# A wait ahead of each indirect DMA: GpSimd issues a fetch or scatter only when the one two places ahead has landed

## The chip, the core and the metric

The kernel runs on one core of a Trainium2 chip. The metric is the device time of one execution in microseconds, as the median of several timed runs. A profile is one further execution, taken with the hardware profiler. The engines are named as the profile names them: PE is TensorE, DVE is VectorE, ACT is ScalarE, POOL is GpSimd and SP is SyncE, which here only issues DMAs.

## What is computed

The input x holds two images of 256 channels and 64 x 64 = 4096 positions, in float32. Two layers follow one another. Cut to what matters:

```
# layer 0
y   = prelu(batchnorm(conv3x3(x)))            # 64 channels
e   = y.reshape(B, 64, N)                     # N = 4096
sim = einsum('bdn,bdm->bnm', e, e)            # 4096 x 4096 for each image
p   = sparsemax(sim, axis=2)                  # max(sim - tau, 0), tau for each row
x   = einsum('bcn,bnm->bcm', x, p) + x
# layer 1
g   = g_w @ x + g_b                           # 128 channels, at each position
a   = w_t . (theta_w @ x + theta_b)           # one number at each position
b   = w_p . (phi_w @ x + phi_b)
f   = relu(a[:, None] + b[None, :] + wf_b)    # 4096 x 4096
y   = (f / N) @ g
x   = batchnorm(wz_w @ y + wz_b) + x
```

In layer 1, f is never needed as a matrix: row n of the product is the sum of (a_n + b_m) g_m over those m with b_m > -a_n. If the positions are sorted by b and running sums of g and b·g are kept in that order, each row is one look-up in the table of sums.

## The kernel before

**A planner orders the work.** Each image passes through the convolution, the search for rows of sim that have more than one entry above the threshold, the rows themselves, the attention product, the projections to g, a and b, and layer 1. The kernel does not write the order down by hand. It describes tasks with `plan.task(cost, fn, rank, after, lat=..., take=..., free=...)`: `cost` has the engine (P, D, A, G for PE, DVE, ACT, POOL; S for SP) and an assumed duration in us, `lat` is an assumed time from its end until others can use the result, `take` and `free` hold a place in a ring of buffers. `Plan.run` plays the tasks through on a clock of its own. On each engine it takes, among the open tasks, the one that could start earliest; when several could start at once, the one of lowest `rank`. Instructions are emitted in the order in which the planner starts them, and each engine runs its own instructions in that order. Costs and ranks so fix the order of the instructions only; on the chip semaphores decide when each one starts. The ranks are the twenty numbers of L281: DB for the mask products on POOL, CV1 for image 1's convolution, RW0 and RW1 for the rows, A0 and A1 for the attention products, R0 and R1 for the sort keys, K0 and K1 for the counting, CH0 and CH1 for the table and the fetches, P1, P2 and SP1 for image 1's projections, PY and PF for its direct product.

**Layer 1 by sorting (class `Ranked`).** Image 0 sorts all 32 tiles of 128 positions, image 1 the first 16; image 1's other 16 tiles go by the direct product (`pair_f` on ACT, L1427; `pair_py` on PE, L1435; `pair_rest`, L1446).

- `above` (L1032 on ACT, L1037 on DVE) and `ties` (L1051) count for each position how many keys come before it; `place` (L1066) turns four tiles' counts into ranks, the `rank` tile.
- `scatter` (L1072) writes a tile's 128 rows of 130 numbers to their ranks in the DRAM table `sg`, by an indirect DMA of POOL. A memset of the one-element tile `gap` (L1071) stands ahead of each. There are 32 for image 0 and 16 for image 1, in groups of four as `place` gives them out. All scatters of an image are declared independent of one another.
- `load` (L1087) brings the sorted table back, `products` (L1098), `sums` (L1105), `before` (L1109) and `raised` (L1112) make the running sums, `stored` (L1118) writes them to the DRAM table `tb`.
- `segments` (L1132, L1133), `places` (L1141) and `counts` (L1150 to L1153) find for each position its place in the table, the tile `k`.
- `fetch` (L1158) is an indirect DMA of POOL which gathers 128 rows of 257 numbers (128 x 257 x 4 bytes) from `tb` into one of the 16 places of the tile `r`. There are 32 for each image. The first 16 of an image follow the stored table; each later one is made a task when the place it overwrites has been used (`taken`, L1192).
- `taken` consumes the fetched rows in blocks of four: `scaled_sums` (L1171, DVE) combines the two halves of a row in place, `turned` (L1178, PE) transposes it, L1183 (image 0, ACT) or L1185 (image 1, DVE) makes `yT`, and `finish` multiplies by wz (`pz`, L956), adds into x (L960, DVE) and stores the block (L963, SP).

POOL also squares conv outputs, makes part of image 1's convolution inputs, multiplies x by a mask (L764, `doubled`) and issues the fetches of the listed rows (L710, L714). In all cases it runs its instructions one after another; the indirect DMAs take turns on eight semaphores.

The planner's entries for the two kinds of DMA:

```
self.fetched[t] = plan.task({"G": 1.27}, lambda: self.fetch(t), rank, after, lat=4.14)
...
self.places_done.append(plan.task({"G": 1.28}, lambda i=i: self.scatter(i), ranked, [pl], lat=2.3))
```

Of the kernel before, what the change touches and what calls it, by code (L numbers as in the profile page):

```python
# [8 lines left out]
F32 = mybir.dt.float32  # L9
# [18 lines left out]
CI = 128  # L28
G = 2
EPS = 1e-5  # L30
HALVINGS = 26
KB = 3
UN = 2 * CB
# [7 lines left out]
TH = 16  # L41
# [5 lines left out]
def both_layers(tc, a, out):  # L47

    nc = tc.nc
    with ExitStack() as keep:
        flag = keep.enter_context(tc.tile_pool(name="flag", bufs=1))
        rows_i = flag.tile([1, 1], I32, name="rows_i")
        sparse_path(tc, a, out, rows_i)
        n = nc.values_load(
            rows_i[0:1, 0:1],
            min_val=0,
            max_val=1 << 16,
            skip_runtime_bounds_check_because="a count of rows",  # L60
        )
        with tc.If(n > 0):
            dense_path(
                tc, a["x"], a["conv_w"], a["vec0"], a["g_wt"], a["g_b"], a["theta_w"], a["phi_w"],
                a["vec_ci"], a["wz_wt"], a["vec1"], out,
            )
# [124 lines left out]
def sparse_path(ctx: ExitStack, tc, a, out, rows_i):  # L191
    nc = tc.nc
# [8 lines left out]
    small = ctx.enter_context(tc.tile_pool(name="small", bufs=1))  # L201
# [44 lines left out]
    def weights():  # L246

        nc.vector.tensor_scalar_add(s1, v1[:, 4, :], EPS)
        nc.scalar.activation(s1, s1, AF.Sqrt)
# [28 lines left out]
            nc.tensor.matmul(pc, lhsT=wc[:, kc], rhs=gw_sb[:, kc], start=(kc == 0), stop=(kc == CT - 1))  # L278
        nc.vector.tensor_sub(gb_sb, gb_sb, pc)

    DB, CV1, LS, RW0, SV1, RW1, A0, G0, A1, R0, K0, CH0, R1, K1, CH1, P1, P2, SP1, PY, PF = 13.5, 11.59, -11.38, -21.22, -11.5, -7.77, 14.5, -12.16, -19.33, 14.33, -0.92, -6.33, -24.95, -6.8, -0.35, -15.83, -22.49, -13.59, 6.76, -7.17  # L281
    plan = Plan()
    ring_sim, ring_av, ring_y, ring_b = Ring(3), Ring(2), Ring(2), Ring(2)

# [650 lines left out]
    def spread(name, column, dst, t0, nt, rank, after):  # L935

        rd, t = as_row(name, column, t0, nt, rank, after)

        def go():
            nc.sync.dma_start(out=dst()[:, ds(t0 * P, nt * P)], in_=rd.to_broadcast((P, nt * P)))  # L940

        return plan.task({"S": 0.1}, go, rank, [t], lat=2.27 + nt * 0.1)
# [33 lines left out]
    class Ranked:  # L976
# [90 lines left out]

        def scatter(self, t):
            b = self.b
            gap = small.tile([1, 1], F32, name=f"gap_{b}_{t}", tag="gap")  # L1070
            nc.gpsimd.memset(gap, 0.0)  # L1071
            rows = nc.gpsimd.indirect_dma_start(  # L1072
                out=self.sg,
                out_offset=bass.IndirectOffsetOnAxis(ap=self.rank[:, t : t + 1], axis=0),
                in_=self.ga[:, t, 0 : CI + 2],
                in_offset=None,
            )

            tc.declare_no_dep(rows.ins, group=f"sg{b}", reason="the ranks are a permutation")
            tc.add_to_no_dep_group(f"sg{b}", rows.ins)  # L1080
# [74 lines left out]
        def fetch(self, t):  # L1155
            if t == 0:
                self.r = self.at("r", [P, TH, CS], F32)
            nc.gpsimd.indirect_dma_start(  # L1158
                out=self.r[:, t % TH],
                out_offset=None,  # L1160
                in_=self.tb,
                in_offset=bass.IndirectOffsetOnAxis(ap=self.k[:, t : t + 1], axis=0),
            )
# [31 lines left out]
            finish(b, ds(i * CB, CB), scaled, "A" if rest is None else "D", rank, after, h)  # L1195

        def fetch_task(self, t, rank, after):
            self.fetched[t] = plan.task({"G": 1.27}, lambda: self.fetch(t), rank, after, lat=4.14)

        def begin(self, rank, after, ranked, chained, then, room):  # L1200

            self.chained, self.then = chained, then
            k = plan.task({"D": 1.65}, self.keys, rank, after)
            hz = ring_b.hold()
            plan.task({"G": 0.2}, self.first, rank, [k], lat=2.3, take=hz, free=[hz])
            sp = spread(f"k{self.b}", lambda: self.key, lambda: self.kb, 0, self.R, rank, [k])
            n = self.R * P
            self.places_done, self.ranked, places = [], [], []
            for t in range(self.R):
                r = ranked + t / 100.0  # L1210
                u = plan.task(
                    {"D": 0.25 + 0.00107 * n, "A": 0.66 + 0.00083 * n}, lambda e, t=t: self.above(t, e == "A"), r, [sp, *room]
                )
                self.ranked.append(u)
                places += [u, plan.task({"D": 0.36}, lambda t=t: self.ties(t), r + 0.02, [sp, *room])]
                if t % 4 == 3:
                    pl = plan.task({"D": 0.6}, lambda t=t: self.place(t - 3), ranked - 0.7, places)
                    for i in range(t - 3, t + 1):
                        self.places_done.append(plan.task({"G": 1.28}, lambda i=i: self.scatter(i), ranked, [pl], lat=2.3))
                    places = []  # L1220
            self.chain()

# [45 lines left out]
    def scales():  # L1268
        nc.vector.tensor_scalar_add(s0, v0[:, 4:5], EPS)
        nc.scalar.activation(s0, s0, AF.Sqrt)  # L1270
        nc.vector.reciprocal(s0, s0)
        nc.vector.tensor_mul(s0, s0, v0[:, 1:2])
        nc.vector.tensor_sub(b0, v0[:, 0:1], v0[:, 3:4])
        nc.vector.tensor_mul(b0, b0, s0)
        nc.vector.tensor_add(b0, b0, v0[:, 2:3])
        nc.vector.tensor_scalar_mul(ns0, s0, -1.0)
# [119 lines left out]
    for m0 in range(0, NT, 6):  # L1396
        early = m0 < 17
        rank = P1 if early else P2
# [5 lines left out]
        after = attended if m0 == 0 else [projected[m0 - 1]]  # L1404
        t = plan.task({"P": 0.37 * 2 * (min(m0 + 6, NT) - m0)}, product, rank, after, take=h)
        t = plan.task({"D": 0.9}, lambda d=d: d["out"](), rank, [t], free=[h])
# [14 lines left out]
    f = []  # L1421

    def pair_f(q, m):
        if not f:
            f.append(room.tile([P, 4, UN], F32, name="f", tag="S2"))
        fm, am, bm = f[0][:, m % 4, :], ab1[0][:, ts(q, UN)], ga1[0][:, m, CI : CI + 1]
        nc.scalar.activation(fm, am, AF.Relu, bias=bm)  # L1427
# [22 lines left out]
    for q in range(NU):  # L1450
        hq = ring_sim.hold()
        for m in range(NR, NT):
            t = plan.task({"A": 1.14}, lambda q=q, m=m: pair_f(q, m), PF, [spread1[q], projected[m]] + prev[-4:-3])
# [25 lines left out]
def dense_path(  # L1479
# [70 lines left out]
    b0 = const.tile([P, 1], F32, name="b0")  # L1550
    nc.vector.tensor_scalar_add(s0, v0[:, 4:5], EPS)
    nc.scalar.activation(s0, s0, AF.Sqrt)
# [8 lines left out]
    b1 = const.tile([P, CT], F32, name="b1")  # L1561
    nc.vector.tensor_scalar_add(s1, v1[:, 4, :], EPS)
    nc.scalar.activation(s1, s1, AF.Sqrt)
# [114 lines left out]
    def search(b, g, z, ntau):  # L1678
# [28 lines left out]
        root = small.tile([P, G], F32, name=f"root_{b}_{g}", tag="root", bufs=1)  # L1707
        with tc.For_i(0, HALVINGS, 1):
            nc.vector.tensor_add(mid, lo, hi)
# [156 lines left out]
```

## Time and profile before

| | us |
|---|---|
| timed runs, median of 3 | 706.8 (706.73, 706.80, 710.09) |
| profiled execution, its own time | 730.27 |
| profiled execution, span from first to last instruction | 728.5 |
| busy PE / DVE / ACT / POOL | 595.0 / 557.5 / 377.1 / 209.5 |
| scatters L1072, 48 of them: first and last start | 425.8 and 547.0 |
| scatter, median duration on POOL | 0.969 |
| fetches L1158, 64 of them: first and last start | 589.7 and 705.1 |
| fetch, median duration on POOL | 0.946 |

How to read it: the span and all times of the trace belong to the profiled execution, which took longer than the timed runs. The duration of an indirect DMA on POOL is that of the instruction; when its data have landed is seen from semaphore events and from who waits for it. In lists of instructions, the bracket at the end of a line holds the idle time of that engine just before it, and what ended it; "issue" means that nothing in the profile was waited for, "remote" or "unknown queue" that the releaser could not be told.

### The profile page before, as it was taken

How to read it: one execution, taken by the hardware profiler on the slowest of the kernel's cores; microseconds unless marked ns; L12 is line 12 of the kernel's file. 1: busy time of each engine (PE TensorE's matmuls, PEld its weight loads, DVE VectorE, ACT ScalarE, POOL GpSimd, SP SyncE). 2: the span in 40 equal slices, each digit the busy share in tenths (PEclk: the TensorE clock that was granted, in tenths of full speed). 3: DMA queues.
4: the chain of work that ended last, by engine and by line, in shares of the span. 5: the costliest groups of instructions: out<-in, count | busy, mean ns of one | idle time of the engine just before them, and what ended most of it. 6: DMA issues, size and time to landing. Idle time of an engine off the chain costs nothing.

```text
span 728.5 us, 7927 instructions
## 1 busy us (share of the span) xinstructions
PE 595.0 (82%) x2629; PEld 291.7 (40%) x2629; DVE 557.5 (77%) x1060; ACT 377.1 (52%) x525; POOL 209.5 (29%) x256
## 2 busy tenths in 40 slices
PE   5998999999688599999965587936999986494983
PEld 4664444444333233444531232624445452242431
DVE  6976877878998988787769999993997974554154
ACT  0123565675366565675035699996983621330500
POOL 0118920000019100000091043433460047456320
PEclk9999999999899799999996789976998989696998
DMA  9621000101200000000110300006504344483253
GB/s 350 207 58 30 1 15 15 30 1 30 87 3 25 1 0 0 1 1 1 59 28 0 146 18 26 26 19 192 154 28 125 143 171 134 130 280 96 58 172 123
DMA packets 32824, 54.42 MB, mean 75 GB/s; under 512 B 12786, under 2 KB 19812, under 8 KB 31876
## 3 DMA queue, kind: packets, MB, share of 16 engines
q1 hardware_dynamic: 27252, 40.60, 16.5%
q0 software_dynamic: 5088, 12.61, 6.4%
q10 hardware_dynamic: 432, 0.59, 0.3%
q8 instruction: 23, 0.38, 0.2%
q14 instruction: 29, 0.24, 0.1%
HBM read 31.62 MB, written 20.07 MB: 71 GB/s over the span
## 4 chain that ended last, share of the span: by engine, by line
PE 48%; DVE 25%; ACT 13%; issue 5%; DMA 3%; another core or an unknown queue 3%; POOL 0%; SPq 0%; DVEq 0%; ACTq 0%
PE sv L476 15%; ACT junk L1032 11%; PE cv_in L363 6%; PE cv_out L363 6%; PE av L838 6%; PE py L1435 5%; DVE junk L1037 3%; PE pz L956 3%; DVE mq L792 2%; PE g L869 2%; DVE xbs L524 2%; DVE a L1020 2%; DVE tab L1105 2%; DVE x L960 1%
## 5 line engine op out<-in xcount | busy, mean ns | idle before, releaser
L528 ACT ACTIVATE sv<-sv,nthr 128x1024 f32<-128x1024 f32 (+1 forms) x131 | 129.0, 984 | 88.0 <-DVE xbs L524 44.3
L524 DVE TENSOR_TENSOR xbs<-sv,xbs 128x1024 f32<-128x1024 f32 (+1 forms) x120 | 130.7, 1089 | 36.5 <-PE sv L476 27.6
L476 PE MATMUL sv<-e 64*128 64x512 f32 x512 | 135.7, 642 | 3.3 <-ACT sv L528 1.8
L1435 PE MATMUL py<-f,ga 128*128 128x512 f32 x256 | 123.0, 632 | 2.3 <-ACT f L1427 2.3
L838 PE MATMUL av<-z,xbs 128*128 128x512 f32 x192 | 99.4, 653 | 22.6 <-DVE x L845 12.0
L1427 ACT ACTIVATE f<-ab,ga 128x1024 f32<-128x1024 f32 x64 | 72.1, 1144 | 88.5 <-PE py L1435 39.7
L1032 ACT ACTIVATE junk<-kb,bound 128x768 bf16<-128x768 f32 (+30 forms) x51 | 94.8, 1859 | 6.4 <-DMA kb<-rd_k 5.8
L1158 POOL DMA_INDIRECT r<-tb,k x64 | 62.5, 977 | 95.5 <-DVE tab L1105 41.7
L1072 POOL DMA_INDIRECT sg<-ga,rank x48 | 50.3, 1047 | 105.8 <-DVE junk L1051 54.5
L1037 DVE TENSOR_SCALAR_CACHE_REDUCE junk<-kb,ga 128x2048 bf16<-128x2048 f32 (+25 forms) x43 | 77.9, 1847 | 2.5 <-DMA kb<-rd_k 1.9
L1435 PEld LDWEIGHTS py<-f,ga 128*128 128x128 f32 x256 | 50.6, 204 | 59.0 <-issue 55.1
L476 PEld LDWEIGHTS sv<-e 64*128 64x128 f32 x512 | 46.0, 195 | 68.0 <-issue 43.4
L838 PEld LDWEIGHTS av<-z,xbs 128*128 128x128 f32 x192 | 35.9, 203 | 79.7 <-issue 47.4
L960 DVE SCALAR_TENSOR_TENSOR x<-pz,s,x 128x512 f32<-128x512 f32 x32 | 22.8, 747 | 42.3 <-PE pz L956 18.4
L363 PE MATMUL cv_out<-v,wu 128*64 128x256 f32 (+1 forms) x384 | 48.9, 394 | 7.6 <-DVE v L325 7.6
L710 POOL DMA_INDIRECT eb<-et,idx x6 | 6.0, 992 | 149.9 <-issue 124.9
L363 PE MATMUL cv_in<-v,wu 128*64 128x256 f32 (+1 forms) x384 | 46.8, 383 | 1.0 <-ACT c L374 1.0
L446 POOL TENSOR_TENSOR sq<-es 128x512 f32<-128x512 f32 x8 | 8.9, 1108 | 133.8 <-ACT es L437 114.0
L363 PEld LDWEIGHTS cv_out<-v,wu 128*64 128x64 f32 x384 | 28.8, 141 | 30.0 <-issue 12.7
L956 PE MATMUL pz<-yT,wz_sb 128*128 128x512 f32 x64 | 31.4, 630 | 6.5 <-DVE yT L1185 4.9
L363 PEld LDWEIGHTS cv_in<-v,wu 128*64 128x64 f32 x384 | 27.8, 136 | 22.1 <-issue 10.7
L533 DVE MAX8 top<-sv 128x8 f32<-128x1024 f32 x29 | 35.5, 1223 | 0.0
(204 smaller groups left out, 761.8 us busy)
## 6 DMA issues: line engine op xcount, KB each, us to landing
out<-x SPq DMA_DIRECT2D x32, 256.0 KB
tb<-tab SPq DMA_DIRECT2D x3, 2056.0 KB
x<-in_x SPq DMA_DIRECT2D x8, 512.0 KB
tab<-sg SPq DMA_DIRECT2D x3, 1040.0 KB
x<-in_x SPq DMA_DIRECT2D x4, 544.0 KB
e<-e SPq DMA_DIRECT2D x16, 128.0 KB
et<-es SPq DMA_DIRECT2D x16, 128.0 KB
mask<-kd SPq DMA_DIRECT2D x2, 1024.0 KB
```

The source lines that it names most:

```text
L363: nc.tensor.matmul(d[jp, g][ts(h, CR), n, (r0 - r) * HH : (r1 - r) * HH], lhsT=taps(j, kc, dy), rhs=v[:, kc, r0 + dy - 1 : r1 + dy - 1], s ...
L476: nc.tensor.matmul(ps[:, ts(h, CB)], lhsT=lhs(h), rhs=e[ts(h, CR), q], start=True, stop=True)
L524: nc.vector.tensor_tensor(out=acc[:, cols], in0=d[i, q][:, cols], in1=acc[:, cols], op=ALU.max)
L528: nc.scalar.activation(ps, ps, AF.Relu, bias=both["nthr"][:, i : i + 1], accum_out=got_s["over"][:, i, q : q + 1])
L838: nc.tensor.matmul(pss[j, ct], lhsT=got["xb"][:, k, ts(ct, P)], rhs=got["zs"][k][:, ts(j, CB)], start=(k == 0), stop=(k == KB - 1),)
L956: nc.tensor.matmul(d["z"][:, ct], lhsT=wz_sb[:, ts(ct, P)], rhs=d["y"], start=True, stop=True)
L1032: nc.scalar.activation(self.junk[:, 0, c0:c1], kb[:, c0:c1], AF.Sign, scale=STEEP, bias=self.bound[:, d, t : t + 1], accum_out=cnt[:, t, 3 ...
L1037: nc.vector.tensor_scalar(self.junk[:, 1, c0:c1], kb[:, c0:c1], self.key[:, t : t + 1], None, (ALU.is_ge, ALU.is_gt)[d], ALU.add, accum_ou ...
L1072: rows = nc.gpsimd.indirect_dma_start(out=self.sg, out_offset=bass.IndirectOffsetOnAxis(ap=self.rank[:, t : t + 1], axis=0), in_=self.ga[: ...
L1158: nc.gpsimd.indirect_dma_start(out=self.r[:, t % TH], out_offset=None, in_=self.tb, in_offset=bass.IndirectOffsetOnAxis(ap=self.k[:, t : t ...
L1427: nc.scalar.activation(fm, am, AF.Relu, bias=bm)
L1435: nc.tensor.matmul(pys[q][:, ts(h, CB)], lhsT=ga1[0][:, m, 0:CI], rhs=f[0][:, m % 4, ts(h, CB)], start=(m == NR), stop=(m == NT - 1),)
```

## The change

Ahead of each scatter but the first two of an image, POOL sets the column of `rank` that the scatter two places ahead used to zero. Since that scatter reads the column as its row numbers, the memset has to wait until it has landed. Ahead of each fetch from t = 2 on, POOL copies one element of the place of `r` that the fetch two places ahead fills into a one-element tile; the copy has to wait for that fetch's landing. POOL runs in order, so the DMA behind the memset or copy waits too. In the task list the cost of a fetch goes from 1.27 to 1.85 and that of a scatter from 1.28 to 1.85, and the ranks are new but for LS and G0. No other instruction is added or taken away.

```
+AHEAD = 2
...
-    DB, CV1, LS, RW0, SV1, RW1, A0, G0, A1, R0, K0, CH0, R1, K1, CH1, P1, P2, SP1, PY, PF = 13.5, 11.59, -11.38, -21.22, -11.5, -7.77, 14.5, -12.16, -19.33, 14.33, -0.92, -6.33, -24.95, -6.8, -0.35, -15.83, -22.49, -13.59, 6.76, -7.17
+    DB, CV1, LS, RW0, SV1, RW1, A0, G0, A1, R0, K0, CH0, R1, K1, CH1, P1, P2, SP1, PY, PF = -22.9, 15.14, -11.38, -27.3, -11.45, -7.46, -2.41, -12.16, -5.23, 8.29, 14.84, -6.15, 5.49, -5.8, -0.65, 8.59, -23.58, -18.61, 8.29, -15.14
...
         def scatter(self, t):
             b = self.b
+            self.sent.append(t)
             gap = small.tile([1, 1], F32, name=f"gap_{b}_{t}", tag="gap")
             nc.gpsimd.memset(gap, 0.0)
+            if len(self.sent) > AHEAD:
+                nc.gpsimd.memset(self.rank[0:1, ds(self.sent[-1 - AHEAD], 1)], 0)
...
         def fetch(self, t):
             if t == 0:
                 self.r = self.at("r", [P, TH, CS], F32)
+            if t >= AHEAD:
+                tick = small.tile([1, 1], F32, name=f"fetched_{self.b}_{t}", tag="gap")
+                nc.gpsimd.tensor_copy(tick, self.r[0:1, (t - AHEAD) % TH, 0:1])
...
-            self.fetched[t] = plan.task({"G": 1.27}, lambda: self.fetch(t), rank, after, lat=4.14)
+            self.fetched[t] = plan.task({"G": 1.85}, lambda: self.fetch(t), rank, after, lat=4.14)
...
+            self.sent = []
...
-                        self.places_done.append(plan.task({"G": 1.28}, lambda i=i: self.scatter(i), ranked, [pl], lat=2.3))
+                        self.places_done.append(plan.task({"G": 1.85}, lambda i=i: self.scatter(i), ranked, [pl], lat=2.3))
```

## The prediction, made before the change was run

> **What bounds the kernel now.** I read the page first (shares, chain by engine), then the chain of waits in order of time, then the waits of the stretches that stood out, then the timeline of POOL.
>
> The page's head, POOL's busy tenths, the chain by engine, and the two groups that the change touches:
>
> ```profile
> span 728.5 us, 7927 instructions
> ...
> POOL 0118920000019100000091043433460047456320
> ...
> PE 48%; DVE 25%; ACT 13%; issue 5%; DMA 3%; another core or an unknown queue 3%; POOL 0%; SPq 0%; DVEq 0%; ACTq 0%
> ...
> L1158 POOL DMA_INDIRECT r<-tb,k x64 | 62.5, 977 | 95.5 <-DVE tab L1105 41.7
> L1072 POOL DMA_INDIRECT sg<-ga,rank x48 | 50.3, 1047 | 105.8 <-DVE junk L1051 54.5
> ```
>
> POOL holds 0% of the chain: its pace limits nothing as a whole. But the chain has 3% of "unknown", unusual on one core. In order of time it is two pieces, both while fetches run:
>
> ```profile
> 610.75 15.92 another core or an unknown queue
> ...
> 658.78 6.68 another core or an unknown queue
> ...
> 674.51 20.60 PE py L1435 x48
> ```
>
> The waits from 605 to 630 us name no releaser either:
>
> ```profile
> DVE x L960 <- remote: 15.9, 1, 15.9
> PEld yr L1178 <- DVE r L1171: 14.7, 1, 14.7
> ...
> ACT f L1427 <- remote: 13.5, 1, 13.5
> ```
>
> VectorE and ScalarE wait, TensorE waits for VectorE. What both wait for is TensorE: its last product before the gap started at 613.87, and in the trace the semaphore events of that work come in one bunch at 626.6 to 626.8. POOL meanwhile goes on, until it runs out of fetches it may issue:
>
> ```profile
> 589.68 0.97 POOL L1158 DMA_INDIRECT r<-tb,k  x1 [41.68 <-DVE tab L1105]
> 590.96 0.97 POOL L1158 DMA_INDIRECT r<-tb,k  x1 [0.30 <-issue]
> ...
> 622.03 0.95 POOL L1158 DMA_INDIRECT r<-tb,k  x1 [0.30 <-issue]
> 626.92 0.94 POOL L1158 DMA_INDIRECT r<-tb,k  x1 [3.93 <-remote]
> ...
> 681.12 0.95 POOL L1158 DMA_INDIRECT r<-tb,k  x1 [0.30 <-issue]
> 701.36 0.94 POOL L1158 DMA_INDIRECT r<-tb,k  x1 [19.30 <-PE yr L1178]
> ...
> 705.11 0.95 POOL L1158 DMA_INDIRECT r<-tb,k  x1 [0.30 <-issue]
> ```
>
> So the stall goes with unbroken bursts of fetches, one per 1.25 to 1.28 us. The second one is alike: burst to 662.8, release at 665.46.
>
> **Is the stall in the timed runs?** This decides the forecast. The profiled execution took 730.27 us (span 728.5 and 1.8 around it), the timed median is 706.8: 23.5 less. The two stalls are 15.92 + 6.68 = 22.6. A timed run without them is 707.7 by this trace, 0.9 from the median. A second sign: of the 16 landing events of a fetch the trace holds 1 to 5 in most of these bursts, but 10 to 16 for 35 of the 48 scatters[...]. I take it at 3 to 1 that recording makes most of the stall.
>
> [...]
>
> **The change, part by part.**
>
> (1) *The wait ahead of each fetch* (62 of 64; t = 0 and 1 have none). Price of landing, issue to the reader's start, where VectorE waits for just this fetch:
>
> ```profile
> 677.37 0.95 POOL L1158 DMA_INDIRECT r<-tb,k  x1 [0.30 <-issue]
> ...
> 680.28 0.35 DVE L1171 SCALAR_TENSOR_TENSOR r<-r,a 128x128 f32<-128x128 f32 x1 [0.99 <-DMA r<-tb,k]
> ```
>
> 2.91; its neighbours 2.86. The copy of one element is new; nearest row, the one-element memset of a scatter:
>
> ```profile
> 428.14 0.09 POOL L1071 MEMSET gap<- 1x1 f32 x1
> 428.44 0.97 POOL L1072 DMA_INDIRECT sg<-ga,rank  x1 [0.22 <-issue]
> ```
>
> 0.09 and 0.22 to the issue. So a fetch starts 2.86 + 0.31 = 3.17 after the one two ahead: 1.58 each. From 640 to 656, while L963 stores the output, the trace's landings come 3.0 to 4.2 after issue instead of 2.4 to 2.8; with some ten fetches at 1.9, the mean is (54 x 1.58 + 10 x 1.9)/64 = 1.63. Bounds: 1.43 if the copy sees the landing as early as its event (2.45 + 0.1 + 0.31 = 2.86, halved), 1.85 as the task list counts. Queued behind the wait on POOL are only further fetches; L1171 waits for them and, as it overwrites what the copy reads, for the copy too (0.1, beside TensorE's work).
>
> (2) *Where that pace lands.* 63 steps from first fetch to last take 102.7. In the trace they take 705.11 - 589.68 = 115.4, less 22.6 is 92.8. The cover was the 19.30 that POOL waits for TensorE ahead of the last four; without the stalls TensorE reaches that point earlier and most of this is gone. Then POOL is the bound of the last 100 us. After the last fetch: 2.86 landing, 0.35 L1171, 0.3 turn, 0.68 yT, 3.7 for four pz, 1.41 x, and 8.4 from the last x (720.09) to the span's end: 17.7 if only its own block is left, 728.5 - 705.11 = 23.4 as now. First fetch of a timed run: 706.8 - 1.8 - 23.4 - 92.8 = 588.8.
> Sum: 588.8 + 102.7 + 17.7 + 1.8 = **711.0**; 716.7 with the long tail. I take the short one: the list now counts slow fetches and has no reason to leave three blocks for the end.
>
> (3) *The wait ahead of each scatter* (all but the first two of an image): a memset on a past column of ranks. The trace's scatters land 2.1 to 2.5 after issue: (2.3 + 0.05 + 0.31)/2 = 1.33 against 1.28. They come in groups of four, and POOL idled 105.8 us between groups: near 0. Some near 498 us landed after 4.5 to 6.3; the next group came at 515, so that hides too. Lower bound 0; upper 3 x 0.6 = 1.8 for each image's last group, as the load (L1087) waits for it. Taken: 0.3, inside the rounding.
>
> (4) *Preferences.* They decide only between tasks that are ready together. By value, the mask products on POOL now precede scatters (DB 13.5 to -22.9), image 0's table steps precede image 1's counts by a hair (CH0 -6.15, K1 -5.8; before -6.33, -6.8) but for the running sums, ranked 0.5 later; most other pairs keep their order. What an order can be worth shows here:
>
> ```profile
> 370.80 14.61 POOL L764 TENSOR_TENSOR x<-x,mask 128x1024 f32<-128x1024 f32 x7
> ...
> 372.81 12.64 DVE L1020 COPY a<-ga 128x32 f32<-128x32 f32 x1
> 385.49 0.18 DVE L1021 TENSOR_SCALAR a<-a 128x32 f32<-128x32 f32 x1
> ```
>
> A copy of 0.18 stands 12.64 behind POOL's masks, on the chain. Bounds: -12.5 if that goes; above, +14 if image 0's products and segments (2 x 2.29 and 8 x 1.2) come ahead of image 1's counts with no gain. Taken: 0, since the masks still are ready at that point and now come no later.
>
> **The rivals.**
> - *The stall is in the timed runs, and the waits end it: faster.* Place: the fetch bursts; price: 22.6. Then the timed first fetch is at 706.8 - 1.8 - 23.4 - 115.4 = 566.2, and the result 566.2 + 102.7 + 17.7 + 1.8 = 688 (694 with the long tail). It decides from the point where the timed runs hold more than 4 to 10 us of stall (711.0 or 716.7 less 706.8). For: the profile shows it. Against: 730.27 - 706.8.
> - *The pace is hidden.* At 1.50 or less per fetch: 588.8 + 94.5 + 19.5 = 703 to 707, no change. For: events land after 2.45. Against: readers start at 2.86. The case that the added waits find everything landed, because POOL is held by TensorE anyway, ends here too.
> - *The wait costs what the list counts*, 1.85, POOL alone the bound: 588.8 + 116.6 + 17.7 + 1.8 = 725.
>
> **How the numbers follow.** 0.5% is 3.5 us, about what a measurement of this kernel can tell from no change. Forecast 0.55, its own range 704 to 722 (about 0.10 of it within 3.5 us); stall removed 0.25; hidden 0.12, half faster by a little; 1.85 each 0.08. Slower 0.45 + 0.08 = 0.53, same 0.10 + 0.06 + 0.01 = 0.17, faster 0.24 + 0.06 = 0.30. The range, 690 to 723, takes in half of the stall case and leaves out the most of 1.85; the bounds of (4) lie within it.
>
> **What would show it.** Profile after: no "remote" wait over 3 us (else the change didn't do it); L1158 about 1.6 apart with POOL's semaphore waits between; span near 710, so that profiled and timed times agree within some 3 us. Wrong if the timed run falls as the profiled one does (the stall was real), or if fetches start 10 us earlier or later than 589 (the order matters).

## The result: 2.8% slower, and the profile after

The changed kernel took 728.5 us (median of 4 runs, 726.4 to 729.0) beside 707.7 us for the kernel before on the same chip: ratio 1.028, 95% interval 1.025 to 1.032, so 20.8 us more where the forecast had 4.2 more. Its profiled execution took 728.7 us with a span of 727.0, so profile and timed runs agree.

From the page of the changed kernel: the head, POOL's busy tenths, the chain by engine, the chain by line, and the three groups that the waits touch (in a group: busy us and mean ns, then the engine's idle time before it and what ended most of it).

```profile
span 727.0 us, 8112 instructions
...
POOL 0118920000029000000191042452440266546650
...
PE 46%; DVE 18%; ACT 14%; DMA 13%; issue 7%; POOL 1%; POOLq 0%; SPq 0%; DVEq 0%; ACTq 0%
...
L1165 POOL DMA_INDIRECT r<-tb,k x64 | 64.2, 1003 | 39.5 <-issue 23.0
L1076 POOL DMA_INDIRECT sg<-ga,rank x48 | 50.6, 1054 | 120.5 <-DVE rank L1067 74.2
L1178 DVE SCALAR_TENSOR_TENSOR r<-r,a 128x128 f32<-128x128 f32 x64 | 21.7, 349 | 41.4 <-POOL fetched L1164 40.2
```

The unknown queue is gone from the chain. In its place DMA holds 13% (3% before), and POOL still only 1%: what is on the chain is not POOL's own work, but what POOL waits for. The waits, in all, times and longest, name it for both engines:

```profile
POOL fetched L1164 <- DMA r<-tb,k: 24.8, 35, 4.6
...
DVE r L1178 <- POOL fetched L1164: 40.2, 29, 5.4
```

How the loop runs is best seen on the chain of waits in order of time (start, us, what). One whole turn of it, late in the fetches:

```profile
652.71 2.78 DMA r<-tb,k
655.49 0.02 issue
...
655.53 0.08 issue
655.62 0.18 POOL fetched L1164
655.80 0.48 issue
656.28 0.67 POOL r L1165
```

A fetch lands 2.78 us after its issue. 0.12 us later POOL's copy starts, takes 0.18, and 0.48 us after its end the next fetch starts. That is 3.57 us for one turn with two fetches in it. POOL's timeline shows the turn from the other side:

```profile
671.38 0.98 POOL L1165 DMA_INDIRECT r<-tb,k  x1 [0.48 <-issue]
672.37 0.18 POOL L1164 COPY fetched<-r 1x1 f32<-1x1 f32 x1
672.93 0.98 POOL L1165 DMA_INDIRECT r<-tb,k  x1 [0.39 <-issue]
674.34 0.18 POOL L1164 COPY fetched<-r 1x1 f32<-1x1 f32 x1 [0.42 <-DMA r<-tb,k]
675.00 0.98 POOL L1165 DMA_INDIRECT r<-tb,k  x1 [0.48 <-issue]
```

671.38 to 675.00 is 3.62 for two, 1.81 a fetch where nothing disturbs. Over all: the first fetch starts at 580.06 and the last at 708.14, so 63 steps take 128.1 us, **2.03 each** (1.63 in the forecast).

### The profile page after: what moved, and what is told of

Same layout as the page of the kernel before. It is cut to its first block, busy times and chain, and to the rows that moved or that the text cites. A ratio compares the mean times of both kernels' runs of the same rounds, so it can differ in the third digit from the quotient of the medians.

```text
span 727.0 us, 8112 instructions
## 1 busy us (share of the span) xinstructions
PE 610.5 (84%) x2629; PEld 293.0 (40%) x2629; DVE 546.2 (75%) x1046; ACT 388.2 (53%) x544; POOL 228.0 (31%) x360
## 4 chain that ended last, share of the span: by engine, by line
PE 46%; DVE 18%; ACT 14%; DMA 13%; issue 7%; POOL 1%; POOLq 0%; SPq 0%; DVEq 0%; ACTq 0%
PE sv L477 15%; ACT junk L1033 11%; DMA r<-tb,k 8%; PE cv_in L364 6%; PE cv_out L364 6%; PE av L839 5%; PE py L1443 3%; PE pz L957 3%; PE g L870 2%; DMA kb<-rd_k 2%; DVE junk L1038 2%; DVE a L1021 2%; DVE xbs L525 2%; DVE mq L793 2%; DVE tab L1116 1%
## 5 line engine op out<-in xcount | busy, mean ns | idle before, releaser
L1443 PE MATMUL py<-f,ga 128*128 128x512 f32 x256 | 127.0, 641 | 3.8 <-ACT f L1435 3.8
L839 PE MATMUL av<-z,xbs 128*128 128x512 f32 x192 | 104.4, 679 | 24.9 <-DVE x L846 13.9
L1033 ACT ACTIVATE junk<-kb,bound 128x256 bf16<-128x256 f32 (+31 forms) x60 | 105.9, 1765 | 10.6 <-DMA kb<-rd_k 9.9
L1165 POOL DMA_INDIRECT r<-tb,k x64 | 64.2, 1003 | 39.5 <-issue 23.0
L1038 DVE TENSOR_SCALAR_CACHE_REDUCE junk<-kb,ga 128x512 bf16<-128x512 f32 (+25 forms) x34 | 65.6, 1967 | 3.8 <-DMA kb<-rd_k 3.4
L1178 DVE SCALAR_TENSOR_TENSOR r<-r,a 128x128 f32<-128x128 f32 x64 | 21.7, 349 | 41.4 <-POOL fetched L1164 40.2
L957 PE MATMUL pz<-yT,wz_sb 128*128 128x512 f32 x64 | 38.0, 740 | 4.3 <-DVE yT L1192 4.3
L364 PEld LDWEIGHTS cv_out<-v,wu 128*64 128x64 f32 x384 | 28.9, 141 | 29.8 <-issue 12.7
L790 ACT COPY z<-rw 128x1024 f32<-128x1024 f32 x24 | 22.9, 1029 | 23.3 <-PE rw L477 23.3
```

The costliest lines, as they stand in the source:

```text
L364: nc.tensor.matmul(d[jp, g][ts(h, CR), n, (r0 - r) * HH : (r1 - r) * HH], lhsT=taps(j, kc, dy), rhs=v[:, kc, r0 + dy - 1 : r1 + dy - 1], s ...
L839: nc.tensor.matmul(pss[j, ct], lhsT=got["xb"][:, k, ts(ct, P)], rhs=got["zs"][k][:, ts(j, CB)], start=(k == 0), stop=(k == KB - 1),)
L957: nc.tensor.matmul(d["z"][:, ct], lhsT=wz_sb[:, ts(ct, P)], rhs=d["y"], start=True, stop=True)
L1033: nc.scalar.activation(self.junk[:, 0, c0:c1], kb[:, c0:c1], AF.Sign, scale=STEEP, bias=self.bound[:, d, t : t + 1], accum_out=cnt[:, t, 3 ...
L1038: nc.vector.tensor_scalar(self.junk[:, 1, c0:c1], kb[:, c0:c1], self.key[:, t : t + 1], None, (ALU.is_ge, ALU.is_gt)[d], ALU.add, accum_ou ...
L1165: nc.gpsimd.indirect_dma_start(out=self.r[:, t % TH], out_offset=None, in_=self.tb, in_offset=bass.IndirectOffsetOnAxis(ap=self.k[:, t : t ...
```

## The experiments

Two theories stood against each other. **P**: the time is set by the pace at which POOL can issue fetches once it waits. **O**: the new costs and preferences bring a worse order. For each kernel the table gives the first fetch's start, the mean step over 63 steps, the time from the last fetch's start to the end of the span, the span, and the ratio of its timed runs to the kernel before on the same chip. The kernel before appears with a second profile of it, explained below.

| kernel | first fetch | step | last to end | span | ratio [95%] |
|---|---|---|---|---|---|
| before, second profile | 589.8 | 1.50 | 23.6 | 708.0 | |
| changed | 580.1 | 2.03 | 18.9 | 727.0 | 1.028 [1.025, 1.032] |
| new order, no waits | 580.5 | 1.40 | 36.2 | 704.8 | 0.992 [0.990, 0.995] |
| old order, fetch waits | 590.2 | 2.14 | 20.8 | 745.8 | 1.049 [1.046, 1.052] |
| old order, scatter waits | 590.6 | 1.51 | 23.3 | 709.0 | 0.999 [0.998, 1.000] |
| spare column | 580.6 | 2.07 | 18.9 | 729.7 | 1.025 [1.021, 1.030] |
| three ahead | 581.5 | 1.58 | 24.9 | 705.9 | 0.997 [0.993, 1.001] |
| new preferences, old costs | 584.8 | 1.71 | 23.6 | 715.9 | 1.009 [1.005, 1.012] |
| old preferences, new costs | 591.1 | 1.40 | 34.2 | 713.4 | 1.005 [1.001, 1.009] |
| fixed pace, longer | 579.1 | 2.25 | 18.4 | 739.1 | 1.044 [1.041, 1.047] |
| fixed pace, shorter | 577.8 | 1.88 | 21.1 | 717.5 | 1.014 [1.012, 1.015] |
| memset in the spare column | 578.6 | 1.97 | 19.0 | 721.5 | 1.017 [1.014, 1.020] |
| memset on the index | 579.7 | 1.85 | 20.9 | 717.1 | 1.009 [1.006, 1.011] |

**New order, no waits.** Both conditions that guard the added instructions are switched off; costs and preferences stay.

```
-            if t >= AHEAD:
+            if False and t >= AHEAD:
```

> The changed kernel with its two waits taken out and all else kept (longer costs, new preferences, so the new order). Theory P: the 20.8 us come from the pace at which GpSimd can issue the 64 fetches once it waits (2.03 us a fetch against about 1.5 without). The order alone starts the fetches 9.6 us earlier (580.1 against 589.7), so 580 + 63 x 1.45..1.6 + 18..24 + 2 = 692 to 707 us, and the profile shows the long stall of the waits on an unrecorded queue again, with a profiled execution 10 us or more above the timed ones. Rival O: the new order is what costs, and the waits are nearly free: 722 to 729 us.

706.4 us beside 711.0. O falls: the new order is 0.8% faster than the old one, and it is the waits that cost. P's time holds, but not by the parts that it gave: the step is 1.40 instead of 1.45 to 1.6, and 36.2 us are left behind the last fetch instead of 18 to 24. Nor did the stall come back, as P had guessed: the span is 704.8, with no unnamed wait. Here the fetches are done at 668.6, long before the end, and from 580 on the chain, by line, is TensorE's (cut off by the view's own width):

```profile
by line: PE py L1443 38.4%; PE pz L957 24.7%; DVE x L961 7.8%; DMA tab<-sg 7.6%; PE yr L1185 5.1%; PE pk L1145 4.9%; DVE r L1178 2.9%; issue 2.8%; DVE yT L1192 2.1%; DVE oh L1137 0.6%; DVE oh L1136 0.4%; PE po L1113 0.3%; DVE tab L1109 0.3%
```

The same view of the changed kernel from 580 on:

```profile
by line: DMA r<-tb,k 40.9%; issue 12.7%; PE pz L957 12.5%; PE py L1443 9.0%; DVE x L961 3.6%; POOL fetched L1164 3.5%; POOL r L1165 3.3%; PE pk L1145 2.2%; DVE r L1178 2.1%; PE yr L1185 1.9%; DVE yT L1192 1.8%; PE po L1113 0.3%; DVE tab L11
```

Landing, issue gaps and the copy hold 57% of that stretch, where TensorE's products held 63%.

**Old order, fetch waits alone.**

```
+            if t >= AHEAD:
+                tick = small.tile([1, 1], F32, name=f"fetched_{self.b}_{t}", tag="gap")
+                nc.gpsimd.tensor_copy(tick, self.r[0:1, (t - AHEAD) % TH, 0:1])
```

> The kernel before with the fetch's wait alone (old costs, old preferences, scatters as they were). Theory P: first fetch near 589, 63 steps of 1.8 (quiet pairs of the changed kernel) to 2.03 (its mean), then 18 to 24 us and 2 us around the span: 722 to 743 us, worse than or equal to the changed kernel's 728.5; the profiled span lies within 3 us of the timed runs and there is no long stall. Rival O (the order costs): 705 to 711 us.

746.3 us, 4.9% slower, 3 us above the top of what P gave: the step is 2.14, as one more stop of 9.6 us stands in it at 710. The waits cost this order more than the new one; the new costs and preferences make up for part of what the waits take.

**Old order, scatter waits alone.**

```
+            if len(self.sent) > AHEAD:
+                nc.gpsimd.memset(self.rank[0:1, ds(self.sent[-1 - AHEAD], 1)], 0)
```

> The kernel before with the scatter's wait alone. Theory P: the scatters lie 80 us or more ahead of the fetches they feed and GpSimd has room there: 706 to 710 us, and the long stall stays in the profile, as the bursts that make it are those of the fetches. Rival S (the scatter's wait delays the last image's ranks and with them the first fetch): 711 to 716 us. Rival R (the scatters fill the recording): the stall is gone from the profile.

710.5 beside 711.0: the scatter's wait costs nothing that these runs can tell. POOL waited 6.3 us for landings, four times, where it otherwise idles. P was wrong on the stall, which is not in this profile. That was rival R's sign, but it says nothing for R, since a second profile of the kernel before has no stall either (below).

**Spare column.** The copy reads a column that VectorE does not overwrite.

```
-                nc.gpsimd.tensor_copy(tick, self.r[0:1, (t - AHEAD) % TH, 0:1])
+                nc.gpsimd.tensor_copy(tick, self.r[0:1, (t - AHEAD) % TH, CI : CI + 1])
```

> The changed kernel in which GpSimd's one-element copy reads column 128 of the fetched rows in place of column 0. VectorE's scaled sum writes columns 0 to 127 in place, so it need not wait until GpSimd has copied. Theory W: VectorE's wait for that copy (40.2 us over the 64 in the profile of the changed kernel, 0.1 in the prediction) is part of the loss: 715 to 723 us. Rival L: the sum's wait is only what remains of waiting for the rows, and the pace is set by landing plus GpSimd's own 0.66 us of copy and issue: 726 to 730 us, with VectorE's wait now put down to the rows' DMA.

730.5 us; its ratio and the changed kernel's overlap. Theory W falls. VectorE's row for the scaled sums shows where the 40.2 us went:

```profile
L1178 DVE SCALAR_TENSOR_TENSOR r<-r,a 128x128 f32<-128x128 f32 x64 | 21.8, 349 | 50.2 <-DMA r<-tb,k 50.1
```

The releaser changed from the copy to the DMA, the wait did not shrink. The wait on the copy in the changed kernel is only the last of two events that come 0.3 us apart.

**Three ahead.**

```
-AHEAD = 2
+AHEAD = 3
```

> The changed kernel with three transfers in flight in place of two (AHEAD = 3, for fetches and scatters). In the changed kernel a fetch starts 3.15 us of landing plus 0.94 us of wake, copy and issue after the fetch two places ahead, so every 2.05 us. Theory P (that loop sets the pace): with three in flight the loop gives (3.15 + 0.94) / 3 = 1.36 us a fetch, which is below the 1.67 us a group that everything else took in the same order without waits (704.8 - 19 - 580.6 over 63), so the time falls back to 704 to 711 us and VectorE's wait on the copy nearly goes. Rival G (each copy on GpSimd or each wait costs by itself, however far back it looks): 720 us or more.

707.4 us: not to be told from the kernel before (0.993 to 1.001), and 21 us under the changed kernel. Rival G falls. The waits are still there, one place further back (each image has one fewer of each kind). What cost was the depth of two. VectorE's wait on the copy fell from 40.2 to 12.7 us; it did not nearly go, as P had said. The step came out at 1.58 rather than the loop's 1.36, because the rest of the work now holds it: from 580 to the end PE py and PE pz lead the chain again with 35.1% and 23.9%.

**Preferences and costs apart.** No waits in either. In the first the two costs go back to the old values, in the second the line of preferences does:

```
-            self.fetched[t] = plan.task({"G": 1.85}, lambda: self.fetch(t), rank, after, lat=4.14)
+            self.fetched[t] = plan.task({"G": 1.27}, lambda: self.fetch(t), rank, after, lat=4.14)
```

> No waits; the new preferences with the old costs of 1.27 and 1.28 us in the list. If the preferences alone give the earlier first fetch (9.6 us) and the 0.8% of the order without waits, then 703 to 709 us. If it is the longer costs that move the list, the kernel goes back to before: 709 to 713 us. If neither works without the other: above 713 us.

> No waits; the old preferences with the new costs of 1.85 us. Costs alone: if the costs move the list, 703 to 709 us with the first fetch near 580; if the preferences do, 709 to 713 us with the first fetch near 590.

716.6 and 713.7 beside 709.6: each alone loses 0.5 to 0.9%, both together win 0.8%. The first lies where neither was to work without the other, the second 0.7 us above both of its ranges. So neither of them is "the" gain. With the old costs a second fetch has to wait for its table's store (45.6 us in two waits instead of 12.7 in one), with the old preferences the first fetch stays at 591.

**Fixed pace.** The new order, no wait for any landing; POOL does three small operations of its own ahead of each fetch.

```
+            fill = small.tile([P, 16], F32, name=f"fill_{self.b}_{t}", tag="fill")
+            nc.gpsimd.memset(fill, 0.0)
+            nc.gpsimd.tensor_scalar(fill, fill, 0.0, None, op0=ALU.mult)
+            nc.gpsimd.tensor_scalar(fill, fill, 0.0, None, op0=ALU.mult)
```

> The new order with no wait for a landing; ahead of every fetch GpSimd does a small memset and two small tensor_scalar operations on a buffer of its own (0.09 + 2 x 0.28 us by the rows of the profile), so that it issues a fetch about every 1.85 us whatever the landing. Theory Pace (only how fast GpSimd can issue counts): first fetch 580.6 + 63 x 1.85 + 19 + 2 = 718 us, and in general 63 times the step that the profile shows above 601.6. Rival Couple (what costs is that each late landing, 5 to 7 us beside a store, stops the next issue): close to the kernel without waits, 704 to 710 us, as long as the step stays under 1.9.

741.9 us. The operations cost more than I had added up; POOL's timeline shows why: each starts 0.08 after the one before has ended, and the fetch 0.43 after the last:

```profile
717.19 0.14 POOL L1163 MEMSET fill<- 128x16 f32 x1
717.41 0.26 POOL L1164 TENSOR_SCALAR fill<-fill 128x16 f32<-128x16 f32 x1
717.75 0.25 POOL L1165 TENSOR_SCALAR fill<-fill 128x16 f32<-128x16 f32 x1
718.44 1.01 POOL L1166 DMA_INDIRECT r<-tb,k  x1 [0.43 <-issue]
...
720.68 1.01 POOL L1166 DMA_INDIRECT r<-tb,k  x1 [0.43 <-issue]
```

With the step that came out, 2.248, Pace's rule gives 601.6 + 63 x 2.248 = 743.2, against the 741.9 measured. No fetch waits for the landing two places back here, and the kernel is slower still than the changed one. Couple had named 704 to 710 only for a step under 1.9, so this run does not decide on it; the next one does.

**A shorter fixed pace**, with one of the two tensor_scalar operations left out:

> As the kernel with a fixed pace, with one of its two small tensor_scalar operations: the step falls by 0.34 us (from one operation's start to the next's), from 1.96..2.25 to 1.62..1.91 us. Theory Pace: first fetch 579 + 63 x step + 19 + 2, so 702 to 720 us and close to 600 + 63 times the mean step of its profile, unless that falls under 706, where the rest of the work is the bound. Rival (GpSimd's operations disturb VectorE, whatever the pace): about half of the 32 us that two of them cost, 723 us or more.

720.0 us at a step of 1.88. Pace's rule gives 600 + 63 x 1.884 = 718.7. The rival asked for 723 or more, and Couple, with the step under 1.9, for 704 to 710: both fall. From 1.88 to 2.25 the span grows by 21.6 us, and 63 x 0.364 is 22.9: nearly one for one. From 1.58 (three ahead, 705.9) to 1.40 (no waits, 704.8) it hardly moves. The bend is between 1.58 and 1.85.

**A memset in place of the copy**, first in the spare column, then on the index that the landed fetch has read:

```
-                nc.gpsimd.tensor_copy(tick, self.r[0:1, (t - AHEAD) % TH, 0:1])
+                nc.gpsimd.memset(self.r[0:1, (t - AHEAD) % TH, CI : CI + 1], 0.0)
```

> The changed kernel in which the wait for the landing hangs on a one-element memset into the spare column 128 of the earlier row (which the rows' readers don't use), in place of a one-element copy out of it. In the changed kernel 0.78 us go by from the landing to the next fetch's start: 0.12 until the copy starts, 0.18 for the copy, 0.48 until the fetch starts. In the scatters the memset starts 0.24 us ahead of its DMA and lasts 0.09. Theory H (the prediction's 0.31 us was right for a memset and wrong for a copy): the handshake is 0.12 + 0.24 = 0.36 us, the loop (3.15 + 0.36 + 0.16) / 2 = 1.83 us a fetch or less, so 580 + 63 x 1.6..1.83 + 19 + 2 = 706 (where the rest of the work is the bound) to 717 us. Rival H0 (any instruction that waits for a landing costs this): 725 to 730 us.

723.4 us, between the two theories, since it was not one kind of handshake but two. In half of the run (the last 16 fetches of each image) the next fetch got a wait on the memset and then, where nothing else delayed it, started 0.6 us after the memset's end; where it got none, 0.15 us. POOL's timeline has both:

```profile
664.01 0.09 POOL L1163 MEMSET r<- 1x1 f32 x1 [0.47 <-DMA r<-tb,k]
664.25 0.94 POOL L1164 DMA_INDIRECT r<-tb,k  x1 [0.15 <-issue]
...
671.61 0.09 POOL L1163 MEMSET r<- 1x1 f32 x1 [0.25 <-DMA r<-tb,k]
672.31 0.94 POOL L1164 DMA_INDIRECT r<-tb,k  x1 [0.61 <-POOL r L1163]
```

So the place of the memset was moved:

```
+                nc.gpsimd.memset(self.k[0:1, ds(t - AHEAD, 1)], 0)
```

> The changed kernel with the fetch's wait hung on a one-element memset into the index column that the earlier fetch has read (as the scatter's wait is), so that no later fetch has to wait for the memset itself. With the memset in the spare column, the fetches that carried no wait on it (those 40 to 47) started 0.05 + 0.09 + 0.15 = 0.29 us after the landing, the others 0.76 us. Theory H (the handshake is 0.3 us for a memset with nothing waiting on it, 0.78 for the copy): the loop is (3.15 + 0.3 + 0.16) / 2 = 1.8 us a fetch with the changed kernel's mean landing and 1.55 with the quiet 2.8, so 580 + 63 x 1.6..1.8 + 19 + 2 = 706 to 714 us, some 10 us or more under the copy's 728. Rival H0 (a wait for a landing costs 0.76 us or more whatever carries it): 722 to 730 us.

718.3 us, ratio 1.009. POOL's timeline, two turns:

```profile
667.49 0.09 POOL L1163 MEMSET k<- 1x1 uint32 x1 [0.53 <-DMA r<-tb,k]
667.73 0.94 POOL L1164 DMA_INDIRECT r<-tb,k  x1
668.86 0.09 POOL L1163 MEMSET k<- 1x1 uint32 x1 [0.19 <-DMA r<-tb,k]
669.10 0.94 POOL L1164 DMA_INDIRECT r<-tb,k  x1 [0.15 <-issue]
670.57 0.09 POOL L1163 MEMSET k<- 1x1 uint32 x1 [0.53 <-DMA r<-tb,k]
670.81 0.94 POOL L1164 DMA_INDIRECT r<-tb,k  x1 [0.15 <-issue]
```

667.73 to 670.81 is 3.08 for two fetches, against 3.62 with the copy. H0 falls. H is right on the handshake (0.24 from memset to fetch) and 4 us short on the time: the mean step is 1.85, not 1.8 or less, since the landings took 3.31 in the mean. Of the changed kernel's loss half to two thirds goes with the copy: 10 us by the medians (728.5 and 718.3), 14 by what each lost to the kernel before on its own chip (20.8 and 6.5). And this kernel, whose fetches wait, has at a step of 1.85 the span of the shorter fixed pace, whose fetches don't, at 1.88 (717.1 and 717.5): of these two the pace decides, whatever makes it.

What the two kernels don't separate is the copy and what the copy waits for. All copies write one one-element buffer (the tag `gap`), so a copy waits for the landing and for POOL's own earlier write of that buffer: in the trace all 60 copies carry both waits, 59 of the 60 memsets on the index the landing's alone. In the views by line, the copies' line (changed kernel) has a semaphore instruction for each copy, the memsets' line (memset on the index) has none:

```profile
L1164 POOLq EVENT_SEMAPHORE  x60: 17/17/17, 583.3 to 707.1; - x60
L1164 POOL COPY fetched<-r x60: 178/178/1818, 583.4 to 707.5; 1x1 f32<-1x1 f32 x60
...
L1163 POOL MEMSET k<- x60: 88/88/89, 583.0 to 695.9; 1x1 uint32 x60
```

Nor is the copy's handshake a plain sum of its parts: in 47 of the 60 turns the next fetch starts 0.78 to 0.80 after the landing, also in 13 in which the copy began 0.21 to 0.39 after it instead of 0.12. With the memset in the spare column the fetch has a wait on POOL's own write, and it took 0.75. So it may be that second wait that costs, and not the copying; a copy into a buffer of its own was not run, and this stays open.

**The kernel before, once more**, for the stall of its first profile.

> The kernel before, unchanged, profiled once more. If the stall of 22.6 us on an unrecorded queue, which made its profiled execution 730 us against 707 in the others, belongs to that one execution: a span of 705 to 711 us without it. If recording makes it each time: a span of 725 us or more with waits on the unrecorded queue again.

709.7 us, span 708.0. POOL's timeline at the two ends of the fetches:

```profile
589.83 1.07 POOL L1158 DMA_INDIRECT r<-tb,k  x1 [41.88 <-DVE tab L1105]
...
680.69 0.94 POOL L1158 DMA_INDIRECT r<-tb,k  x1 [14.22 <-PE yr L1178]
...
684.44 0.94 POOL L1158 DMA_INDIRECT r<-tb,k  x1 [0.30 <-PE pz L956]
```

The same fetches in 94.6 us instead of 115.4, and no wait without a named releaser; nor is there one in any of the other twelve profiles taken since, with or without waits. The stall belonged to one execution. That the recording made it was the author's estimate, at 3 to 1, and was not shown: the same bursts of 1.25 us a fetch were recorded here and in the new order without waits, and nothing stopped.

## Why the prediction was wrong, step by step

**The stall** was rightly kept out, though that the recording makes it, the reason given, was not shown. The kernel without it was put together from the stalled trace as first fetch 588.8, 92.8 for the steps, 23.4 behind; the second profile has 589.8, 94.6 and 23.6.

**The sum**, first fetch + 63 steps + what is left + 1.8, only divides the time, so it closes for any kernel; its terms show where the forecast failed. For the changed kernel it is 580.1 + 128.1 + 18.9 + 1.7 = 728.8. Term by term against the forecast: first fetch -8.7, steps +25.4, last part +1.2. That POOL's pace becomes the bound of the last 100 us was right, and the experiments with a fixed pace show it.

**The step that failed is (1), the price of the wait.** It was put at 2.86 + 0.31 for a turn of two fetches, with stores 3.26. In the trace's semaphore events, as a mean of the 60 turns with a copy, it is 4.11: the last landing event 3.21 after issue, 0.25 to the copy, 0.22 for the copy, 0.43 to the next fetch. (There are 60 and not 62, as the first two fetches of each image have none. The expectations above put 3.15 and 0.94 for landing and the rest; with the last event of every fetch counted it is 3.21 and 0.90.)
- The larger part is the handshake, that is all from the landing to the next fetch's start: 0.90 against 0.31, which is 0.59 / 2 x 60 = 17.7 us. The nearest row was that of a memset, and for a memset with one wait it was right: 0.29 was measured with the memset on the index. But the change makes a copy, with a second wait. There it is 0.78 even where nothing else delays it, and the rest of the 0.90 is other delays met at that point (the first copy alone lasts 1.82 us).
- The landing itself is the smaller part: 3.21 against 2.95 with the stores counted in, so 0.26 / 2 x 60 = 7.8 us. Of the 60, 39 landed in under 3.0 us (mean 2.83) as forecast, but late landings come often. Two fetches issued at 626.8 and 628.2 landed after 7.0 and 6.6, beside the table's 2 MB store tb<-tab, issued at 627.4. Twelve more between 634 and 699 took 3.3 to 4.8; the last four of them lie beside eight stores of 256 KB, issued within 8.2 us from 690.8. In the kernel before such late landings (mean 3.45 in its second profile) did not hold POOL back.
- The lower bound of 1.43 rested on the first of the landing events (2.45). The wait ends with the last. In the trace of the changed kernel 63 of the 64 fetches have sixteen landing events; for the 60 that a copy waits for, the first comes 2.74 after issue in the mean and the last 3.21. No copy starts earlier than 0.12 after the last, and 37 of the 60 start within 0.01 of that.
- The upper bound, 1.85, was the list's own cost, a number that somebody chose for the planning and not a measurement. It was no bound.

**VectorE's wait for the copy** was put at 0.1 and is 40.2 us in the waits, but the price was nearly right: with the spare column the time stays, as VectorE then waits for the landing instead.

**Where the pace lands (2):** the short last part was right (18.9 for 17.7).

**The scatters (3)** at next to nothing: right.

**The preferences (4)** at nothing: not so. The first fetch starts 9.8 us earlier than in the second profile, within the bound of 12.5 but not through the copy behind the masks: that copy stays, 14.8 us in place of 12.6. What the 9.8 us come from was not traced. In time the new order gives 0.8% without the waits. Step (4) weighed the preferences alone, and the runs show that they work only together with the costs. It also took them to decide on the order only. But for the counts (`above`) the task list leaves the engine open too: wherever the new preferences are in, 9 of the 94 count instructions moved from VectorE to ScalarE, with the new costs alone none. So that no other instruction is added or taken away is true of the code, not of what each engine runs.

**The rivals.** The stall in the timed runs fell. The hidden pace: that is what three ahead shows, and two ahead does not. Each wait at 1.85: the nearest in time with 725, but by two errors that nearly cancel, a step 0.18 too short (11 us) and a first fetch 8.7 us too late.

## What to carry to other kernels

A wait for the landing of the transfer n places back turns latency into pace: a step of (landing + handshake) / n, as measured here for n = 2: (3.21 + 0.90) / 2 = 2.05, beside a mean step of 2.03. Where that was above what the readers needed, nearly every step counted in full (21.6 us of 22.9 between the two fixed paces); here n = 3 came out even with the kernel before and n = 2 cost 2.8%. Price the handshake by the very instruction that carries it, with everything that this instruction waits for, and the landing by its mean with the stores around, not by a quiet one. Before reading a stall without a releaser as the kernel's, profile it a second time. The version that is faster than both kernels is the new order without waits: 706.4 us, 0.992 [0.990, 0.995] of the kernel before.

## What the runs showed of the hardware that was not expected

- On POOL, how a wait is carried matters: from landing to the next indirect DMA's start it took 0.29 us with a one-element memset that has this wait alone, 0.75 with a memset where the DMA also waits on it, 0.78 with a one-element copy that also waits for POOL's own earlier write.
- Two stops of 15.9 and 6.7 us stood in one profile of a kernel and not in its second one, nor in any of its variants.
- In the stretch from 580 to 620 us the granted clock of TensorE was 0.74 in the changed kernel, 0.87 in the same order without waits, and 0.91 with three ahead, though PE was busy for 35.1, 36.6 and 34.8 of 40 us. Why was not tried.
